# Key-tile weights added by accumulating DMA, and matmuls of one kind gathered by beat, in a two-layer graph-attention kernel

## The chip, the cores and the metric

The kernel runs on one core of a Trainium2 chip. Time is device microseconds of one launch. Three runs of the kernel before gave 4396.21, 4403.12 and 4403.44 us, so the median is 4403.12 us. The profile is that of one more execution, which took 4387.29 us; its span, from the first to the last recorded instruction, is 4385.5 us, with a mean granted TensorE clock of 0.98.

## What is computed

Two layers over `x` of shape [8, 2048, 256] (8 batches, 2048 nodes, 256 features) with one adjacency matrix of 2048 x 2048. Cut to what matters here:

```python
# layer 0: four heads of 64; a softmax over each chunk of 256 keys, the chunks' results are added
scores = einsum("bhnd,bhjcd->bhnjc", q, k) / sqrt(64)
scores = where(mask == 0, -10, clip(scores, -10, 10))
ctx = einsum("bhnjc,bhjcd->bhnd", softmax(scores, axis=-1), v)
x = layernorm(x + layernorm(ctx @ Wo.T + bo + x) * gamma + beta)
# layer 1: graph attention, one head
Wh = x @ W
e = where(adj or eye, leaky_relu(s_i[:, None] + s_j[None, :], 0.2), -inf)
x = layernorm(x + elu(softmax(e, axis=-1) @ Wh))
```

## The kernel before

**Layer 0** works on blocks of 512 queries (`ib`, 4 per batch) and chunks of 256 keys (`j`, 8 per block), 256 chunks in all. A chunk has two halves, one key tile of 128 each, and a half is a *beat*. The loop over `J` and `half` writes out the order of every engine by hand: each engine executes what the program gives it in that order. Keys lie on the partitions, queries along the free axis. In its beat a key tile gets its scores (line 899, two PSUM tiles `sc` of two heads each, from a ring of two), the cap by the mask on VectorE (909) and the exponential on ScalarE (912), which makes the two weight tiles `e` of 128 x 1024. The four `e` of a chunk come from a ring of eight.

One chunk later the weights of chunk `prev` are used (928): a matmul with `ones` as stationary operand gives the sum over the keys (part 2), two with the values give the halves of the head's features (parts 0 and 1). Each takes both key tiles (`i` = 0, 1), accumulates in PSUM, and uses a strip of 32 columns per head. The even beat does parts 2 and 0, the odd beat part 1. The results go to SBUF by ScalarE (936 to `un`, 942 to `ds`), both through a PSUM ring of two, `m`. The sums go by DMA to a compact tile (944), are inverted on VectorE (950), go to DRAM and come back spread over the partitions (952, 956); two beats after the sums `scaled` multiplies `un` (963, VectorE) and adds it to `ctxT` (964, GpSimd).

**Layer 1** of batch b runs beside layer 0 of batch b+1. A *step* is one key tile of a block of 512 queries; 16 steps make a block, four blocks a batch. A step has five parts on four engines: `low` (714, ScalarE), `leaky` (718, VectorE), `edges` (723, VectorE), `weights` (727, an exponential on ScalarE, then the add to `acc` on GpSimd, 736) and `product` (746, four matmuls into the one PSUM tile `us`; for the last batch 761). After the 16th product ScalarE copies `us` to `hx` (773), and the next block's first product has to wait for that copy. A step's `w` comes from a ring of five. `begin_beat` adds 1.5 steps of credit per beat (`RATE`), so beats alternate between one new step and two; the parts are spread so that `low` is in beat n, `leaky` and `edges` in n+1, `weights` and `product` in n+2. Within a beat the order is: `weights`, `low`, `leaky` (in `begin_beat`), then scores, caps and exponentials of layer 0, then `edges`, then the matmuls on `prev`, then `end_beat`: the products, one turn of each generator in `ahead` (the preludes: `Wh`, and the row maxima in `half_max`, 438) and `fins` (projections, the ends of blocks), and the agenda.

Layer 0 ends before layer 1 does. The last loop, `while agenda or fins or ...`, then runs beats with no scores in them: one step a beat for what is left of batch 6 and all 64 steps of batch 7.

All DMAs are issued by SyncE. GpSimd's queue has only arithmetic.

Of the kernel before, what the change touches and what calls it, by code (L numbers as in the profile page):

```python
# [9 lines left out]
F32 = mybir.dt.float32  # L10
# [4 lines left out]
ALU = mybir.AluOpType  # L15
# [4 lines left out]
P = 128  # L20
# [8 lines left out]
def tile_adj_attention__then__gat(  # L29
# [35 lines left out]
    nc = tc.nc  # L65
    B, N, F = x.shape
    H, D = 4, 64
# [3 lines left out]
    IB = 512  # L71
    NIB = N // IB
# [17 lines left out]
    four = ctx.enter_context(tc.tile_pool(name="four", bufs=4))  # L90
    five = ctx.enter_context(tc.tile_pool(name="five", bufs=5))
    eight = ctx.enter_context(tc.tile_pool(name="eight", bufs=8))
# [136 lines left out]
    for n in range(2):  # L229
        t = one.tile([P, F], F32, tag=("hx", "ex")[n], name=f"a_bc{n}")  # L230
        nc.sync.dma_start(out=t, in_=a[n * F : (n + 1) * F, :].rearrange("f o -> (f o)").partition_broadcast(P))
        a_bc.append(t)
# [355 lines left out]
    def fin1(b, ib, hx, acc):  # L588

        hr = one.tile([P, TPB, F], F32, tag="hr", name=f"hr{b}_{ib}")  # L590
        nc.sync.dma_start(out=hr, in_=h_d[b, ib])
        yield


        pr = ps_m.tile([P, TPB], F32, tag="m", name=f"pr{b}_{ib}")
        for t in range(TPB):
            nc.tensor.matmul(pr[:, t : t + 1], acc[:, ts(t, P)], ones[:, 0:1], start=True, stop=True)
        r = two.tile([P, TPB], F32, tag="r1", name=f"r1{b}_{ib}")
        nc.vector.reciprocal(r, pr)
        for t in range(TPB):  # L600
            nc.scalar.activation(hx[:, t, :], hx[:, t, :], AF.Identity, bias=ones[:, 0:1], scale=r[:, t : t + 1])
        ex = one.tile([P, TPB, F], F32, tag="ex", name=f"ex{b}_{ib}")
        nc.scalar.activation(ex, hx, AF.Exp, bias=shifts[:, 1:2])
        yield
        nc.vector.scalar_tensor_tensor(hx, ex, 1.0, hx, ALU.min, ALU.max)
        nc.gpsimd.tensor_add(hx, hx, hr)
        yield
        mv, rstd = yield from stats(hx, f"c{b}_{ib}")
        yield
        normalize(hx, mv, rstd, f"c{b}_{ib}")  # L610
        nc.sync.dma_start(out=out[b, ts(ib, IB), :].rearrange("(t p) f -> p t f", p=P), in_=hx)

    def fin1_last(b, ib, hx):
# [3 lines left out]
        nc.sync.dma_start(out=hr, in_=h_d[b, ib])  # L617
        ex = one.tile([P, TPB, F], F32, tag="ex", name=f"ex{b}_{ib}")
        st = two.tile([P, TPB, 6], F32, tag="st", name=f"st_c{b}_{ib}")
# [84 lines left out]
    class Step:  # L704
# [6 lines left out]
        def low(self):  # L711
            k, c = self.k, self.c
            self.w = five.tile([P, IB], F32, tag="w", name=f"w{self.name}")
            nc.scalar.activation(self.w, k["ab"][:, 1, :], AF.Identity, bias=k["sj"][:, 1, c : c + 1])  # L714
# [98 lines left out]
    def at(when, fn):  # L813
        agenda.setdefault(when, []).append(fn)

    def begin_beat(rate):
        nonlocal l1_live, credit, lows, edged, weighted, leaking
        weighted, edged = edged, []
        for s in weighted:
            s.weights()  # L820
        leaking, lows = lows, []
        credit = min(credit + rate, 2.0)
        while l1_live and credit >= 1.0:
            s = next(l1, False)
            if s is False:
                l1_live = False
            elif s is None:
                break
            else:
                credit -= 1.0  # L830
                lows.append(s)
                s.low()
        for s in leaking:
            s.leaky()

    def middle_of_beat():
        nonlocal edged
        for s in leaking:
            s.edges()
        edged = leaking  # L840

    def end_beat():

        nonlocal weighted
        if beat < 2 * NIB * NCH or beat >= 2 * total:
            for fn in agenda.pop(beat, []):
                fn()
        for s in weighted:
            s.product()
        weighted = []  # L850
        for gens in (ahead, fins) if beat < 2 * total else (fins, ahead):
# [17 lines left out]
    fins.append(far_made())  # L869

    prev = None
    mk0 = {}
    for J in range(total + 1):
        b, ib, j = J // (NIB * NCH), J // NCH % NIB, J % NCH
        live = J < total
        if live and j == 0:
            ctxT = one.tile([P, 2, IB], F32, tag="ctx", name=f"ctxT{b}_{ib}")
        cur = {"b": b, "ib": ib, "j": j, "es": [], "ctxT": ctxT, "v": vs[min(b, B - 1)], "name": f"{b}_{ib}_{j}"}
        for half in range(2):
            c = 2 * j + half  # L880
            if live:
# [6 lines left out]
                if c % HT == 1:  # L888
                    n = (b * NIB + ib) * 2 + c // HT + 1
                    nb, nib, nhf = n // (2 * NIB), n // 2 % NIB, n % 2  # L890
                    if 0 < nb < B:
                        mk0[nb, nib, nhf] = mask_block(0, nib, nhf, f"{nb}_{nib}_{nhf}")
            begin_beat(RATE if b < B - 1 else LAST_RATE)
            if live:
                scs = []
                for hp in range(NPAIR):
                    sc = ps_s.tile([P, 2, IB], F32, tag="sc", name=f"sc{b}_{ib}_{c}_{hp}")
                    for h in range(2):
# [6 lines left out]
                        )  # L905
                    scs.append(sc)
                cap = mk[:, c % HT, :].unsqueeze(1).to_broadcast([P, 2, IB])
                for hp in range(NPAIR):
# [6 lines left out]

            early = J < NIB * NCH
            if prev is not None:
                if half == 0:

                    pool, tag = (one, "hr") if early and J % 3 == 2 else (two, "un")  # L920
                    prev["un"] = pool.tile([P, 2, IB], F32, tag=tag, name=f"un{prev['name']}")
                for part in ((2, 0), (1,))[half]:
                    m = ps_m.tile([P, IB], F32, tag="m", name=f"u{prev['name']}_{part}")
                    for i in range(2):
                        pc = 2 * prev["j"] + i
                        for h in range(H):
                            f0 = h * D + part * DH
                            nc.tensor.matmul(  # L928
                                m[h * DH : (h + 1) * DH, :],
                                prev["v"][pc // TPB][:, pc % TPB, f0 : f0 + DH] if part < 2 else ones[:, 0:DH],  # L930
                                prev["es"][2 * i + h // 2][:, h % 2, :],
                                start=(i == 0),
                                stop=(i == 1),
                            )
                    if part < 2:
                        nc.scalar.copy(prev["un"][:, part, :], m)  # L936
                    else:

                        ds = two.tile([P, IB], F32, tag="ds", name=f"ds{prev['name']}")
                        nc.scalar.copy(ds, m)  # L942
                        dc = two.tile([P, IB // DH], F32, tag="dc", name=f"dc{prev['name']}")
                        nc.sync.dma_start(
                            out=dc, in_=ds.rearrange("(h m) (n w) -> h m n w", m=DH, n=DH)[:, 0, :, :]
                        )
                        prev["dc"] = dc

                        def inverse(p=prev):
                            nc.vector.reciprocal(p["dc"], p["dc"])  # L950
                            p["rd"] = dram3.tile([H, IB], F32, tag="rd", name=f"rd{p['name']}")
                            nc.sync.dma_start(out=p["rd"].rearrange("h (m w) -> (h m) w", m=DH), in_=p["dc"])

                        def spread(p=prev):
                            p["r"] = two.tile([P, IB], F32, tag="r", name=f"r{p['name']}")
                            nc.sync.dma_start(out=p["r"], in_=p["rd"].unsqueeze(1).to_broadcast([H, DH, IB]))

                        def scaled(p=prev):
                            r2 = p["r"].unsqueeze(1).to_broadcast([P, 2, IB])
                            if p["j"] == 0:  # L960
                                nc.vector.tensor_mul(p["ctxT"], p["un"], r2)
                            else:
                                nc.vector.tensor_mul(p["un"], p["un"], r2)  # L963
                                nc.gpsimd.tensor_add(p["ctxT"], p["ctxT"], p["un"])  # L964
                            if p["j"] == NCH - 1:
                                ctx_done[p["b"], p["ib"]] = beat
                            if p["j"] == NCH - 3:
                                fins.append(fin(p["b"], p["ib"], p["ctxT"]))

                        lag = 1 if early else 0  # L970
                        at(beat + lag, inverse)
                        at(beat + lag, spread)
                        at(beat + 2 + 2 * lag, scaled)

            end_beat()
            if half == 1:

# [8 lines left out]
    while agenda or fins or ahead or l1_live or l1_open():  # L986
        begin_beat(1.0)
        middle_of_beat()
        end_beat()
        beat += 1  # L990
# [44 lines left out]
```

## Time and profile before

| | us |
|---|---|
| median of three runs | 4403.12 |
| the profiled execution | 4387.29 |
| its span | 4385.5 |
| PE busy | 4064.2 (93%) |
| VectorE (DVE) busy | 3417.7 (78%) |
| ScalarE (ACT) busy | 2564.4 (58%) |
| GpSimd (POOL) busy | 1760.5 (40%) |
| DMA, share of the 16 engines' span | 30.5% for queue q1, which SyncE feeds |

An fp32 matmul of the program is two MATMUL and two LDWEIGHTS instructions in the profile, so the scores of a beat (four matmuls) are eight. Busy time is time with an instruction in flight; PE's instructions overlap, so a group's mean duration is longer than its share of the busy time. A timeline gives start, duration, engine, line, operation, tiles and count of each stretch of like instructions; in brackets stands how long the engine was idle before and what released it.

### The profile page before, as it was taken

How to read it: one execution, taken by the hardware profiler on the slowest of the kernel's cores; microseconds unless marked ns; L12 is line 12 of the kernel's file. 1: busy time of each engine (PE TensorE's matmuls, PEld its weight loads, DVE VectorE, ACT ScalarE, POOL GpSimd, SP SyncE). 2: the span in 40 equal slices, each digit the busy share in tenths (PEclk: the TensorE clock that was granted, in tenths of full speed). 3: DMA queues.
4: the chain of work that ended last, by engine and by line, in shares of the span. 5: the costliest groups of instructions: out<-in, count | busy, mean ns of one | idle time of the engine just before them, and what ended most of it. 6: DMA issues, size and time to landing. Idle time of an engine off the chain costs nothing. (4 is left out here: it accounts for less than half of the span.)

```text
span 4385.5 us, 61171 instructions
## 1 busy us (share of the span) xinstructions
PE 4064.2 (93%) x23053; PEld 1907.6 (43%) x23053; DVE 3417.7 (78%) x4530; ACT 2564.4 (58%) x3842; POOL 1760.5 (40%) x901
## 2 busy tenths in 40 slices
PE   8889989999999999999899999999999999899767
PEld 3223334454344534454344543445434454344456
DVE  5876589965998669976699766996579965888777
ACT  5655556665566556666566665566556665555546
POOL 0222235543455334444245442554325542354420
PEclk9999999999999999999999999999999999999889
DMA  5554232222332233321333223232232222322321
GB/s 166 182 163 149 71 115 86 83 73 89 99 90 81 64 107 102 100 75 51 105 102 98 74 74 105 85 95 78 70 106 85 89 78 67 115 83 80 123 73 58
DMA packets 257641, 415.63 MB, mean 95 GB/s; under 512 B 85440, under 2 KB 120512, under 8 KB 256448
## 3 DMA queue, kind: packets, MB, share of 16 engines
q1 hardware_dynamic: 257344, 411.71, 30.5%
q8 instruction: 181, 2.97, 0.3%
q14 instruction: 116, 0.95, 0.1%
HBM read 340.66 MB, written 68.88 MB: 93 GB/s over the span
## 5 line engine op out<-in xcount | busy, mean ns | idle before, releaser
L912 ACT ACTIVATE e<-sc 128x1024 f32<-128x1024 f32 x1024 | 1034.2, 1020 | 1049.9 <-DVE sc L909 1006.7
L909 DVE SCALAR_TENSOR_TENSOR sc<-sc,mk 128x1024 f32<-128x1024 f32 x1024 | 1206.7, 1223 | 538.3 <-PE sc L899 352.6
L899 PE MATMUL sc<-qT,kT 64*128 64x512 f32 x4096 | 1060.4, 633 | 86.7 <-ACT e L912 86.2
L964 POOL TENSOR_TENSOR ctxT<-ctxT,un 128x1024 f32<-128x1024 f32 x224 | 568.5, 2538 | 1145.3 <-DVE un L963 1007.0
L928 PE MATMUL u<-e,v 128*32 128x512 f32 x8192 | 980.9, 597 | 0.0
L746 PE MATMUL us<-wh,w 128*128 128x256 f32 x3584 | 878.6, 395 | 81.9 <-ACT w L727 60.4
L746 PEld LDWEIGHTS us<-wh,w 128*128 128x128 f32 x3584 | 667.7, 193 | 422.2 <-ACT w L727 110.7
L736 POOL TENSOR_TENSOR acc<-acc,w 128x512 f32<-128x512 f32 x392 | 601.7, 1535 | 544.9 <-ACT w L727 534.4
L899 PEld LDWEIGHTS sc<-qT,kT 64*128 64x128 f32 x4096 | 347.2, 189 | 611.6 <-ACT e L912 281.8
L718 DVE SCALAR_TENSOR_TENSOR w<-ab,sj,w 128x512 f32<-128x512 f32 x512 | 571.5, 1137 | 4.6 <-ACT w L714 4.5
L928 PEld LDWEIGHTS u<-e,v 128*32 128x32 f32 x8192 | 240.6, 110 | 659.7 <-issue 543.9
L928 PE MATMUL u<-e,ones 128*32 128x512 f32 x4096 | 497.5, 604 | 0.0
L723 DVE TENSOR_TENSOR w<-w,mk 128x512 f32<-128x512 f32 x512 | 458.6, 917 | 37.1 <-DMA mk<-mask 34.6
L438 DVE CUSTOM_DVE_ANT_0 fb<-sj_row,fb 128x1024 bf16<-128x1024 f32 x240 | 387.8, 1626 | 2.3 <-DMA fb<-far 2.3
L714 ACT ACTIVATE w<-ab,sj 128x512 f32<-128x512 f32 x512 | 352.2, 714 | 8.7 <-POOL acc L734 5.4
L727 ACT ACTIVATE w<-w 128x512 f32<-128x512 f32 x512 | 308.8, 629 | 75.9 <-DVE w L723 75.3
L936 ACT COPY un<-u 128x512 f32<-128x512 f32 x512 | 300.5, 587 | 66.5 <-PE u L928 57.6
L963 DVE TENSOR_TENSOR un<-un,r 128x1024 f32<-128x1024 f32 x224 | 278.1, 1242 | 42.2 <-DMA r<-rd 36.7
L928 PEld LDWEIGHTS u<-e,ones 128*32 128x32 f32 x4096 | 107.8, 110 | 356.5 <-issue 305.4
L950 DVE RECIPROCAL dc<-dc 128x16 f32<-128x16 f32 x256 | 63.9, 249 | 149.8 <-DMA dc<-ds 134.0
L942 ACT COPY ds<-u 128x512 f32<-128x512 f32 x256 | 148.5, 580 | 3.0 <-PE u L928 2.5
L349 POOL TENSOR_TENSOR y<-x,bo_bc 128x1024 f32<-128x1024 f32 x32 | 77.6, 2426 | 163.6 <-DMA x<-in_x_dram 103.0
(112 smaller groups left out, 3114.7 us busy)
## 6 DMA issues: line engine op xcount, KB each, us to landing
r<-rd SPq DMA_DIRECT2D x256, 256.0 KB
mk<-mask SPq DMA_DIRECT2D x120, 512.0 KB
fb<-far SPq DMA_DIRECT2D x240, 256.0 KB
xT_k<-in_xT_dram SPq DMA_DIRECT2D x32, 512.0 KB
raw<-in_adjT_dram SPq DMA_DIRECT2D x32, 512.0 KB
rawf<-in_adj_dram SPq DMA_DIRECT2D x32, 512.0 KB
x<-in_x_dram SPq DMA_DIRECT2D x32, 512.0 KB
h_d<-y SPq DMA_DIRECT2D x32, 512.0 KB
```

The source lines that it names most:

```text
L438: nc.vector.tensor_tensor_reduce(out=fb, in0=row, in1=fb, scale=1.0, scalar=2 * FAR * 0.999, op0=ALU.add, op1=ALU.max, accum_out=dst,)
L714: nc.scalar.activation(self.w, k["ab"][:, 1, :], AF.Identity, bias=k["sj"][:, 1, c : c + 1])
L718: nc.vector.scalar_tensor_tensor(self.w, k["ab"][:, 0, :], k["sj"][:, 0, c : c + 1], self.w, ALU.add, ALU.max)
L723: nc.vector.tensor_tensor(self.w, self.w, self.k["mks"][self.c // HT][:, self.c % HT, :], ALU.min)
L727: nc.scalar.activation(self.w, self.w, AF.Exp)
L736: nc.gpsimd.tensor_add(k["acc"], k["acc"], self.w)
L746: nc.tensor.matmul(k["us"][:, t, :], self.w[:, ts(t, P)], k["wh"][c // TPB][:, c % TPB, 0:F], start=(first and t % 2 == 0), stop=last, ski ...
L899: nc.tensor.matmul(sc[:, h, :], kTs[b][c // TPB][h * D : (h + 1) * D, hp, ts(c % TPB, P)], qT[h * D : (h + 1) * D, hp, :], start=True, sto ...
L909: nc.vector.scalar_tensor_tensor(scs[hp], scs[hp], -CLIP, cap, ALU.max, ALU.min)
L912: nc.scalar.activation(e, scs[hp], AF.Exp)
L928: nc.tensor.matmul(m[h * DH : (h + 1) * DH, :], prev["v"][pc // TPB][:, pc % TPB, f0 : f0 + DH] if part < 2 else ones[:, 0:DH], prev["es"] ...
L964: nc.gpsimd.tensor_add(p["ctxT"], p["ctxT"], p["un"])
```

## The change

It concerns chunks that have layer-1 steps in hand beside them (`together`), found at the start of each even beat. For these:

- The even beat does both value parts of `prev`, key tile by key tile. After them GpSimd issues two DMAs that add the weights of the second key tile to those of the first, in place (128 x 1024 fp32 each).
- The sums of that chunk are taken one chunk later, in the next even beat behind the scores, from the added tiles alone: one key tile in place of two.
- The layer-1 products are held for the odd beat.

For all beats the layer-1 parts are ordered anew: `weights_and_lows` (first the exponentials and the adds to `acc`, then the `low` of the new steps) comes at the end of an even beat, behind the copies of `un`, and at the start of an odd beat. `leaky` and `edges` follow in `begin_beat` and `middle_of_beat`, so a `low` of an odd beat is used in that beat. The last loop calls `weights_and_lows`, `begin_beat`, `middle_of_beat` in this order, too. The rings change: `w` from five to six tiles, `un` from two and a guest in `hr` to three, `ds` from two to one; `fin1` loads `hr` later, and `ex` shares the place of `hr`.

```diff
-    def begin_beat(rate):
-        nonlocal l1_live, credit, lows, edged, weighted, leaking
-        weighted, edged = edged, []
-        for s in weighted:
+    def weights_and_lows(rate):
+        nonlocal l1_live, credit, lows, edged, weighted
+        for s in edged:
             s.weights()
-        leaking, lows = lows, []
+        weighted, edged = weighted + edged, []
         credit = min(credit + rate, 2.0)
...
                 lows.append(s)
                 s.low()
+
+    def begin_beat():
+        nonlocal lows, leaking
+        leaking, lows = lows, []
         for s in leaking:
             s.leaky()
...
-        for s in weighted:
-            s.product()
-        weighted = []
+        if products:
+            for s in weighted:
+                s.product()
+            weighted = []
...
+    def sums(p, lag):
...
+        m = ps_m.tile([P, IB], F32, tag="m", name=f"s{p['name']}")
+        tiles = 1 if p["added"] else 2
+        for i in range(tiles):
+            for h in range(H):
+                nc.tensor.matmul(
+                    m[h * DH : (h + 1) * DH, :],
+                    ones[:, 0:DH],
+                    p["es"][2 * i + h // 2][:, h % 2, :],
...
-            begin_beat(RATE if b < B - 1 else LAST_RATE)
+            early = J < NIB * NCH
+            rate = RATE if b < B - 1 else LAST_RATE
+            if half == 1:
+                weights_and_lows(rate)
+            begin_beat()
+            if half == 0:
+                together = prev is not None and live and bool(leaking or edged or weighted)
...
+            if half == 0:
+                for p in unsummed:
+                    sums(p, 0)
+                unsummed = []
...
+                    if not together:
+                        sums(prev, 1 if early else 0)
+                parts = (0, 1) if together and half == 0 else (half,) if not together else ()
...
+                for i in range(2):
+                    for part, m in zip(parts, ms):
+                        values(prev, part, m, i)
+                    if together and half == 0 and i == 1:
...
+                        for hp in range(NPAIR):
+                            nc.gpsimd.dma_start(
+                                out=prev["es"][hp], in_=prev["es"][NPAIR + hp], accum_op=ALU.add
                             )
+                        prev["added"] = True
+                        unsummed.append(prev)
+                for part, m in zip(parts, ms):
+                    nc.scalar.copy(prev["un"][:, part, :], m)
+            if half == 0:
+                weights_and_lows(rate)
+            edged = edged + leaking
-            end_beat()
+            end_beat(half == 1 or not together)
...
     while agenda or fins or ahead or l1_live or l1_open():
-        begin_beat(1.0)
+        weights_and_lows(1.0)
+        begin_beat()
         middle_of_beat()
-        end_beat()
+        edged = edged + leaking
+        end_beat(True)
         beat += 1
```

## The prediction, made before the changed kernel was run

> **What bounds the kernel now.** The page first: PE is busy 93% of the span, but the slices of its second part do not say the same everywhere.
>
> ```profile
> PE   8889989999999999999899999999999999899767
> DVE  5876589965998669976699766996579965888777
> ```
>
> DVE's digits rise to 9 and fall to 5 once per batch (some 4.7 slices), so two engines may take turns. The list of scores (line 899) in the timeline gives the batches' period, 526 us from batch 3 to batch 4 (1485.7 to 2012.5), 32 chunks. The line-746 products show which chunks have layer 1 beside them: 22 of 32, in batches 1 to 7, so 154 chunks. Busy time of the stages of one period, then of the end (columns: stretch, length, PE, PEld, DVE, ACT, POOL, clock, DMA share, GB/s):
>
> ```profile
> 1660.00:1895.00 235.00, 222.41 (x1294) 106.76 (x1286) 221.50 (x274) 146.33 (x218) 120.15 (x61) 0.99 0.33 99
> 1895.00:2065.00 170.00, 168.21 (x920) 87.07 (x920) 116.44 (x151) 102.30 (x158) 72.06 (x42) 1.00 0.20 60
> 4245.00:4373.00 128.00, 115.33 (x481) 92.01 (x481) 103.06 (x187) 86.33 (x146) 3.02 (x3) 0.96 0.19 66
> ```
>
> In 13 chunks of the first stretch, where the row maxima (438) run, PE and DVE are both at 94%: taking PE work away there leaves DVE. In the 9 chunks of the second PE is alone at 99%. In the third, the end, one layer-1 step comes every 128/60 = 2.13 us.
>
> A plain chunk with three steps, on PE:
>
> ```profile
> 2353.81 1.99 PE L899 MATMUL sc<-qT,kT 64*128 64x512 f32 x8
> ...
> 2355.72 1.92 PE L928 MATMUL u<-e,ones 128*32 128x512 f32 x16
> ...
> 2357.46 1.90 PE L928 MATMUL u<-e,v 128*32 128x512 f32 x16
> ...
> 2359.29 2.00 PE L746 MATMUL us<-wh,w 128*128 128x256 f32 x8
> ...
> 2361.22 1.99 PE L899 MATMUL sc<-qT,kT 64*128 64x512 f32 x8
> ...
> 2363.14 1.92 PE L928 MATMUL u<-e,v 128*32 128x512 f32 x16
> ...
> 2364.99 3.72 PE L746 MATMUL us<-wh,w 128*128 128x256 f32 x16
> ...
> 2368.64 1.99 PE L899 MATMUL sc<-qT,kT 64*128 64x512 f32 x8
> ```
>
> Start to start, PE never rests: 14.83 us.
>
> **What PE is spared.** Sixteen sum instructions become eight: 1.74/2 = 0.87 us. Entering a kind of matmul also costs: the two-part `u` group takes 3.57 us, the one-part 1.85, so 1.72 per part and 0.13 for entry; the products take 3.65 against 1.93, so 1.72 per step and 0.21 for entry. The Trainium skill, "TensorEngine Tiling (Array Packing)", section Key Properties, says that a change of tiling mode drains the array; it names no price, the rows do. The order goes from six kinds a chunk to four (scores, sums with values; scores, products), which drops one `u` and one `us` entry: 0.34 us. Together 1.21, and PE's chunk becomes 13.62 us. Over 154 chunks that would be 186 us, if PE were the bound everywhere.
>
> **What takes its place inside a chunk.** `low` now stands behind the copies of `un`, these behind the values, and `leaky` of all three steps ahead of the odd beat's caps. That closes a ring. From the end of the even scores: sums 0.87 + 0.13, values 3.44, hop and last copy 0.07 + 0.58, three exponentials at 0.54 (start to start), the first `low` 0.71, three `leaky`, two caps 2.35, hop and exponential of the second pair 0.1 + 1.02, hop and scores of that pair 0.1 + 0.96. Without `leaky` 11.95 us. Single `leaky` instructions of the timeline take 0.72 us alone (102 of them) and 1.40 with a POOL instruction in flight at their start (139); the mean of the row is 1.137. This is where the rule that speaks against the change comes in: the Trainium skill, "SBUF — State Buffer", section Who interferes with whom, says a DVE instruction with two SBUF inputs contends with a GpSimd instruction that reads SBUF, and `leaky` is one. The adds to `acc` (1.27 each) start as soon as the exponentials end, and now meet `leaky`. By the rule the ring is 11.95 + 4.20 = 16.2 us, by `leaky` alone 14.1, by the mean 15.4. I take 15.4, since the first add can pass while DVE waits for `low`.
>
> So a PE-bound plain chunk goes from 14.8 to 15.4; one with a projection (3.5 us or more on PE) stays PE's and gains 1.21. In the nine chunks of the second stretch six have such work, two are plain, one has few steps: -7.3 + 1.1 - 0.4 = -6.6 us a batch, **-46 us** for seven. In the 13 chunks of the first stretch (mean 17.1 us) DVE's work stays what it is. Ends: -1.21 x 91 = -110, if DVE's contention shrinks as PE's work does, and +91 if each chunk loses 1 us to the ring. I take **0**.
>
> **Block changes.** `us` is one PSUM tile; the copy to `hx` stands on ACT behind the odd beat's exponentials. Today:
>
> ```profile
> PE us L746 <- ACT hx L773: 21.5, 7, 3.9
> ```
>
> 21.5 us in 7 waits. With three products in one run, the 16th step ends inside the run at two of a batch's three inner boundaries. In the ring's time the second exponential ends 14.3 us after the even scores, the copy (1.01) at 15.4. The first product ends near 8.4. If the boundary follows it, two products (3.45) and scores (1.92) come behind the copy: 20.8 against 15.4, +5.4. If it follows the second: +3.7. 14 such boundaries x 4.55 = 64, less 21.5: **+42 us**; from 0, if the stall falls into DVE's backlog, to 64.
>
> **The end.** There `leaky` used the `low` of the beat before; now it needs that of its own beat, which stands on ACT behind the exponential of the step before, which needs that step's `edges`. The trace shows this very chain once, where it happened to run without slack:
>
> ```profile
> 4298.11 0.70 ACT L714 ACTIVATE w<-ab,sj 128x512 f32<-128x512 f32 x1
> ...
> 4298.85 0.75 DVE L718 SCALAR_TENSOR_TENSOR w<-ab,sj,w 128x512 f32<-128x512 f32 x1 [0.64 <-ACT w L714]
> ...
> 4299.64 0.69 DVE L723 TENSOR_TENSOR w<-w,mk 128x512 f32<-128x512 f32 x1
> ...
> 4300.36 0.63 ACT L727 ACTIVATE w<-w 128x512 f32<-128x512 f32 x1 [0.41 <-DVE w L723]
> 4300.90 0.71 ACT L714 ACTIVATE w<-ab,sj 128x512 f32<-128x512 f32 x1
> ```
>
> From `low` to `low` 2.79 us. At one step a beat, 60 steps x (2.79 - 2.13) = **+40 us**. The ends of blocks (`fin1_last`) fit into DVE's and ACT's gaps of the chain. Bounds: 20 to 55.
>
> **The accumulating DMAs.** No row has one; GpSimd issues none today. Room: from the values' end to the sums, 15.4 - 4.4 = 11 us. Nearest rows: the 8 KB dc<-ds takes 1.81 us in the chain of waits, and in the busiest 20 us (4140 to 4160) 258 GB/s went at a share of 0.73, so 353 GB/s at full share. Two tiles are 1.05 MB: 3.0 us in one pass; if the add reads its target too, two passes, 5.9, over the 0.7 that others leave 8.5; with 1.8 for landing, 4.8 to 10.3. The fit of "DMA: Bandwidth & Descriptors", section Anatomy of one DMA — SWDGE (gpsimd) path (2.0 us plus the bytes over 436,000 a us), would make it 6.4, one after the other. Cost taken: 0, hidden by the odd beat; ends 0 and what rival 2 says. Issuing 308 DMAs on POOL has no row either (SP's issues take 0.3 to 0.56 us each): POOL is busy half of either stretch, and behind the two waiting issues stand only the adds to `acc`, whose exponentials come later. 0, ends 0 and +1 us in each of the 91 DVE-bound chunks, should the issue keep DVE off SBUF as POOL's adds do.
>
> The later sums move dc, rd and r by a chunk; `scaled` moves with them, and nothing but the output projection waits for it, 2 beats later. `hr` in `fin1` is loaded a beat before its use, on SP behind `ex`. 0, ends -5 and +15 over the run.
>
> **Sum.** -46 + 0 + 42 + 40 = +36 us on the profiled 4387.29, so 4423; the three runs lie higher, median 4403.12, and there the same +0.8% gives **4440**.
>
> **Rivals.**
> 1. *PE's saving carries (faster).* If `edges`, now issued where POOL is idle, and `leaky` run at 0.72, the ring is 14.1: plain chunks gain 0.7, and the first stretch gains half of PE's 1.21. -9 a batch and -0.6 x 91: -63 - 55 + 20 (stalls half absorbed) + 40 = -58, so 4345. It decides once the ring is below 14.8 us. For: DVE's singles at 0.72 to 0.75 wherever POOL rests. Against: the `acc` adds sit right there.
> 2. *The DMA lands late.* From 11 us on, the chunk is the landing time + 4.4. At three passes, 12.7 + 1.8 = 14.5, a chunk takes 18.9 at least; of the 22 some 17 are shorter, by 2.5 us on average: +42 a batch, +290, 4730. For: no row excludes it. Against: two passes fit.
>    That `together` holds in fewer chunks than 154 would shrink every term but the end's.
> 3. *The ring is contended.* 16.2 us, +1 in the DVE-bound chunks: plain chunks +1.4, so -34 in the second stretch, +91 + 42 + 40: +139, 4540.
>
> **How the numbers follow.** Forecast 0.45, its own range 4408 to 4500; rival 1 0.25, rival 2 0.16, rival 3 0.14. About 0.2% (9 us) is what a measurement can tell from no change. Faster: all but a little of rival 1, and a part of the forecast's lower side, 0.26; same 0.08; slower 0.66. The range 4335 to 4650 leaves out a part of rival 1 and the worse half of rival 2.
>
> **What would show it.** Right: chunks with projections 1.2 us shorter, plain ones near 15.4 with DVE waiting for line-714 `low`; PE waiting for `hx` 5 and 4 us, twice a batch; steps of the end at 2.8 us; sums that do not wait for a DMA. Wrong: plain chunks below 14.5, or PE waiting at the sums.

## The result, and the profile after

Four runs of the changed kernel gave 4995.81 to 5018.11 us, median 5010.1; four of the kernel before 4396.21 to 4403.44, median 4403.18. The ratio is 1.1379 (95% interval 1.1351 to 1.1407): the change costs some 607 us. The forecast was 4440, and the time lies far above its range.

The slices of the page of the changed kernel, to be read beside the two shown of before, with the granted TensorE clock:

```profile
PE   8889877898788887889888888888987889888666
DVE  6875678665776667766677556776577765777665
PEclk9999989899899998999989998899998999989789
```

PE's row of nines is gone, and DVE no longer swings to 9: where two engines took turns as the bound, now neither is full. The clock falls below 9 all along the run; its mean is 0.926 where it was 0.980. Sums of the page say the same: PE idles 840 us of the span (4994.0 less 4154.0) where it idled 321, and is busy 90 us *longer*, with fewer instructions.

The stages of one period and the end, in the columns of the table shown of before. The first row holds the same chunks of batch 3 as the 235 us of before, the second the nine behind them, the third the products of the last batch:

```profile
1834.00:2107.00 273.00, 220.68 (x1139) 101.76 (x1139) 208.66 (x252) 141.91 (x211) 120.48 (x79) 0.90 0.52 128
2107.00:2304.00 197.00, 173.55 (x873) 92.02 (x873) 132.03 (x165) 105.98 (x160) 94.25 (x62) 0.96 0.44 104
4782.00:4979.00 197.00, 135.50 (x522) 98.39 (x522) 123.09 (x219) 97.52 (x164) 6.89 (x5) 0.95 0.15 48
```

The first stretch grew from 235 to 273 us. DVE was busy 94% of it and is now at 76%; PE executes 155 matmul instructions fewer (104 of them sums; the others have moved to neighbouring chunks) in the same busy time, at a clock of 0.90 where it was 0.99. The second grew from 170 to 197. By the starts of the scores, averaged over batches 2 to 5, a batch went from 527.4 to 609.3 us: its 21 chunks with layer 1 from 377.6 to 444.2, its 11 others from 149.8 to 165.1. (The same places of a batch are compared in every kernel; one of the 11 still holds one or two steps.) From the last scores to the last matmul it was 263 us and is 341.

One plain chunk of batch 4 (on PE it has nothing but scores, sums, values and products) in the timeline of the changed kernel, from even scores to even scores, PE, ACT, POOL and DVE together:

```profile
2507.66 1.99 PE L969 MATMUL sc<-qT,kT 64*128 64x512 f32 x8
...
2510.46 3.71 PE L881 MATMUL u<-e,v 128*32 128x512 f32 x32
...
2514.11 1.99 PE L969 MATMUL sc<-qT,kT 64*128 64x512 f32 x8
2514.24 0.59 ACT L1012 COPY un<-u 128x512 f32<-128x512 f32 x1 [0.22 <-PE u L881]
2514.73 1.67 ACT L728 ACTIVATE w<-w 128x512 f32<-128x512 f32 x3
2515.51 4.30 POOL L737 TENSOR_TENSOR acc<-acc,w 128x512 f32<-128x512 f32 x3 [0.75 <-ACT w L728]
2516.03 5.45 PE L747 MATMUL us<-wh,w 128*128 128x256 f32 x24
2516.30 1.94 ACT L715 ACTIVATE w<-ab,sj 128x512 f32<-128x512 f32 x3
2517.04 6.07 DVE L719 SCALAR_TENSOR_TENSOR w<-ab,sj,w 128x512 f32<-128x512 f32 x3 [3.34 <-ACT w L715]
2519.77 2.79 POOL L924 TENSOR_TENSOR ctxT<-ctxT,un 128x1024 f32<-128x1024 f32 x1
2523.04 2.35 DVE L985 SCALAR_TENSOR_TENSOR sc<-sc,mk 128x1024 f32<-128x1024 f32 x2
2524.29 2.15 ACT L988 ACTIVATE e<-sc 128x1024 f32<-128x1024 f32 x2 [6.06 <-DVE sc L985]
...
2525.37 3.79 PE L969 MATMUL sc<-qT,kT 64*128 64x512 f32 x8 [3.90 <-ACT e L988]
```

This is the ring of the prediction, link by link: values, copies, exponentials, `low`, three `leaky`, caps, exponential, scores. It takes 17.71 us. DVE waits 3.34 us for the first `low`; then three `leaky` take 6.07 us, 2.02 each, while GpSimd has adds in flight (its two lines). Taken one by one in the trace, they last 1.64, 1.75 and 2.83 us. GpSimd's second and third add to `acc` and the larger add of `scaled` (924) end at 2518.14, 2519.81 and 2522.57, and each `leaky` ends some 0.55 us after one of these: the two engines take turns. The forecast had 1.137 each, 1.40 at worst. The odd beat's caps stand behind them; PE has been through with its products for 3.90 us when the exponential lets it go on, and the eight scores instructions that follow take 3.79 us where eight took 1.99. The clock column (the third from the right) says why, in the first part of the wait, in its last part, and in the scores behind it:

```profile
2521.50:2523.50 2.00, 0.00 (x0) 0.00 (x0) 2.00 (x2) 0.00 (x0) 1.07 (x1) 1.00 1.02 274
2523.70:2525.30 1.60, 0.00 (x0) 0.00 (x0) 1.60 (x2) 1.01 (x1) 0.00 (x0) 0.50 0.81 229
2525.37:2529.20 3.83, 3.83 (x12) 1.25 (x16) 3.59 (x10) 1.02 (x1) 0.00 (x0) 0.50 0.08 27
```

Some 2.2 us after PE's last product (2521.48) the granted clock went to one half, and it stayed there while PE worked again.

Waits of the kernel before, then of the changed kernel (engine, tile and line, what it waited for: us in total, times, longest):

```profile
DVE w L718 <- ACT w L714: 4.5, 9, 1.3
...
PE sc L899 <- ACT e L912: 86.2, 57, 6.3
```

```profile
DVE w L719 <- ACT w L715: 530.5, 273, 6.1
...
PE sc L969 <- ACT e L988: 424.2, 139, 7.2
...
PE us L747 <- ACT hx L774: 93.4, 14, 9.7
```

The third was 21.5 us before, in 7 waits. The 14 block changes are where the prediction put them.

The accumulating DMAs, from the list of DMA issues (number, KB each, median us from issue to landing):

```profile
e<-e POOLq DMA_DIRECT2D x302, 512.0 KB, 6.4
```

The two of a chunk together take 8.0 us from the first issue to the last landing (median of 151 pairs), 11.2 at most. 302 are two in each of 151 chunks, so `together` holds about where it was expected (154 chunks), and among what PE's sums wait for there is no DMA.

### The profile page after: what moved, and what is told of

It reads as the page before. It is cut to its first block, busy times and chain, and to the rows that moved or that the text cites. A ratio compares the mean times of both kernels' runs of the same rounds, so it can differ in the third digit from the quotient of the medians.

```text
span 4994.0 us, 59349 instructions
## 1 busy us (share of the span) xinstructions
PE 4154.0 (83%) x21845; PEld 1935.9 (39%) x21845; DVE 3468.9 (69%) x4530; ACT 2582.1 (52%) x3842; POOL 1941.6 (39%) x1203
## 5 line engine op out<-in xcount | busy, mean ns | idle before, releaser
L969 PE MATMUL sc<-qT,kT 64*128 64x512 f32 x4096 | 1195.5, 701 | 458.0 <-ACT e L988 424.2
L719 DVE SCALAR_TENSOR_TENSOR w<-ab,sj,w 128x512 f32<-128x512 f32 x512 | 773.4, 1542 | 534.2 <-ACT w L715 530.5
L747 PE MATMUL us<-wh,w 128*128 128x256 f32 x3584 | 862.2, 397 | 133.2 <-ACT hx L774 93.4
L969 PEld LDWEIGHTS sc<-qT,kT 64*128 64x128 f32 x4096 | 377.7, 205 | 1072.9 <-ACT e L988 691.4
L1006 POOL DMA_DIRECT2D e<-e x302 | 269.5, 1033 | 1196.6 <-PE u L881 1094.4
L737 POOL TENSOR_TENSOR acc<-acc,w 128x512 f32<-128x512 f32 x392 | 549.2, 1401 | 196.6 <-ACT w L728 177.2
L724 DVE TENSOR_TENSOR w<-w,mk 128x512 f32<-128x512 f32 x512 | 382.7, 787 | 79.5 <-DMA mk<-mask 76.7
L905 ACT COPY ds<-s 128x512 f32<-128x512 f32 x256 | 149.4, 583 | 547.8 <-PE s L897 392.5
L897 PE MATMUL s<-e,ones 128*32 128x512 f32 x2888 | 406.9, 666 | 14.6 <-DVE y L364 13.5
L438 DVE CUSTOM_DVE_ANT_0 fb<-sj_row,fb 128x1024 bf16<-128x1024 f32 x240 | 319.3, 1341 | 0.0
L897 PEld LDWEIGHTS s<-e,ones 128*32 128x32 f32 x2888 | 72.3, 115 | 333.7 <-issue 274.5
```

What stands on the lines that cost most here:

```text
L719: nc.vector.scalar_tensor_tensor(self.w, k["ab"][:, 0, :], k["sj"][:, 0, c : c + 1], self.w, ALU.add, ALU.max)
L724: nc.vector.tensor_tensor(self.w, self.w, self.k["mks"][self.c // HT][:, self.c % HT, :], ALU.min)
L737: nc.gpsimd.tensor_add(k["acc"], k["acc"], self.w)
L747: nc.tensor.matmul(k["us"][:, t, :], self.w[:, ts(t, P)], k["wh"][c // TPB][:, c % TPB, 0:F], start=(first and t % 2 == 0), stop=last, ski ...
L897: nc.tensor.matmul(m[h * DH : (h + 1) * DH, :], ones[:, 0:DH], p["es"][2 * i + h // 2][:, h % 2, :], start=(i == 0), stop=(i == tiles - 1),)
L969: nc.tensor.matmul(sc[:, h, :], kTs[b][c // TPB][h * D : (h + 1) * D, hp, ts(c % TPB, P)], qT[h * D : (h + 1) * D, hp, :], start=True, sto ...
```

## The experiments

In the expectations "ring" or "Theory A" is the order of layer 1, A1 the work that ScalarE has between the `low` of a chunk, A2 `leaky` contended by GpSimd, S the lateness of the sums, H the holding of the products for the odd beat, and D the accumulating DMAs. Of each kernel not stated otherwise the rest is that of the changed kernel. "21" and "11" are the us of a batch's chunks with and without layer 1, as above.

### Is it the order or the DMAs?

**No accumulating DMAs**, the late sums over both key tiles:

```diff
-                        for hp in range(NPAIR):
-                            nc.gpsimd.dma_start(out=prev["es"][hp], in_=prev["es"][NPAIR + hp], accum_op=ALU.add)
-                        prev["added"] = True
```

> The changed kernel without the accumulating DMAs: sums still one chunk late, but over both key tiles. Theory A (the ring low - leaky - caps - exponentials - scores - values - copies - low sets the length of a chunk): the DMAs are off the ring and 0.87 us of sums is added to it in 151 chunks, so 5010 to 5140 us. Rival B (the DMAs: landing, or their issue on GpSimd, hold the chunk): clearly below the changed kernel, 4450 to 4700 us.

Measured: 5077.18 us (one run), 21: 452.2. That is in the ring's range. Without the DMAs it is slower still, so neither their landing nor their issue is what costs the 607 us.

**The old order** of layer 1, in the chunks and in the last loop; DMAs, late sums and held products stay:

```diff
-    def begin_beat():
+    def begin_beat(rate):
         nonlocal lows, leaking
-        leaking, lows = lows, []
+        held, lows = lows, []
+        weights_and_lows(rate)
+        leaking = held
...
-            if half == 0:
-                weights_and_lows(rate)
```

> The changed kernel with the layer-1 order of the kernel before (exponentials, then low, then leaky for the low of the beat before, all at the start of every beat, also in the last loop); accumulating DMAs, late sums, values in even beats and products in odd ones stay. Theory A: the ring is open, so the time falls to that of the kernel before or below it, 4250 to 4420 us. Rival B (DMAs): stays above 4700 us. Rival C (holding the products for the odd beat, with the stall for hx at block changes, is the cost): stays above 4600 us.

4525.76 us, ratio to before 1.0283 (1.0266 to 1.03); 21: 383.0, 11: 164.6. The time lies in none of the three ranges: the order carries 484 of the 607 us, but 123 are left that the ring theory did not expect.

**The old order in the last loop only:**

> The changed kernel with the order of the kernel before in the last loop alone. Theory A: the end (64 steps of the last batch, 198 us in the changed kernel against 148 before) is back at about 148 us and the rest stays, so 4930 to 4970 us. If the longer end has another cause than leaky needing the low of its own beat: 4990 to 5010 us.

4947.23 us (one run): the last loop is 63 of the 484; the stretch behind the last scores is 57 us shorter.

**The new order only** (`together = False`, so old sums and values, no DMAs, products in every beat):

> The changed kernel with no chunk taken as together: sums over both tiles at once, values one part a beat, products in every beat, no accumulating DMA; the new layer-1 order stays in all beats. Theory A: nearly the whole loss is the order's, 4850 to 5150 us. Rivals B and C (DMAs, held products): 4400 to 4550 us, the end's 50 us being all that is left.

5108.1 us (one run), 21: 465.5, 11: 161.7 (9.1 of these 11.9 us more are in the one place of the 11 that has steps). It is in the ring's range. The order needs no help from the rest of the change.

### Which part of the ring?

**All `low` of a chunk in the even beat** (`weights_and_lows(2 * rate, 3.0)` there, none in the odd one):

> The changed kernel with all of a chunk's low in the even beat, behind the exponentials, and none in the odd one; leaky for all of them still opens the odd beat, so the ring stays closed. Theory A1 (the ring is longer than forecast because ScalarE's work for block ends and projections stands between the low of the even and of the odd beat): chunks with layer 1 lose 2 to 4 us, 4600 to 4850 us. Theory A2 (because leaky meets GpSimd's adds): 4960 to 5040 us.

4945.72 us (one run), 21: 433.7. Only 64 us come back, in neither range and nearest to A2's: work between the `low` of two beats is a small part.

**The ring cut.** All `low` of a chunk stand in the even beat, as in the kernel above, behind the copies, but their `leaky` and `edges` wait for the next even beat:

```diff
-    def begin_beat():
+    def begin_beat(mine=True):
         nonlocal lows, leaking
-        leaking, lows = lows, []
+        leaking, lows = (lows, []) if mine else ([], lows)
...
-            begin_beat()
+            begin_beat(half == 0)
...
             if half == 0:
-                weights_and_lows(rate)
+                weights_and_lows(2 * rate, 3.0)
```

> The changed kernel with the ring cut: all lows of a chunk stand behind the even beat's copies of un, as before, but their leaky and edges wait for the next even beat, 20 us later, so that no cap stands behind a leaky whose low is fresh. The accumulating DMAs, late sums, held products, the last loop and the place of the lows and step exponentials on ScalarE stay. Ring theory (the way from low through leaky to the caps of the same beat is what makes a chunk with layer 1 last 20 us): such chunks come back near the 383 us per 21 of the old order, and with the last loop's 60 us left the time is 4580 to 4650. Rival, contention alone (leaky takes 1.54 us because GpSimd's adds meet it): at most 3 x 0.4 us per chunk come back, 25 us a batch, so 4830 to 4900. Rival, ScalarE's place alone (step exponentials and lows between the copies and the odd beat's exponentials delay the latter): nothing comes back, 4930 to 5020.

4632.9 us, ratio 1.0542 (1.0515 to 1.057), 21: 388.1. 377 us are gone, inside the ring theory's numbers and far from both rivals'; against the kernel above, which differs in the place of `leaky` and `edges` alone, it is 313. A plain chunk of batch 4, in the timeline of this kernel:

```profile
2103.54 1.99 PE L967 MATMUL sc<-qT,kT 64*128 64x512 f32 x8
...
2111.23 2.37 DVE L983 SCALAR_TENSOR_TENSOR sc<-sc,mk 128x1024 f32<-128x1024 f32 x2 [0.91 <-ACT w L728]
...
2112.18 1.94 ACT L715 ACTIVATE w<-ab,sj 128x512 f32<-128x512 f32 x3
...
2113.51 5.49 DVE L719 SCALAR_TENSOR_TENSOR w<-ab,sj,w 128x512 f32<-128x512 f32 x3
...
2117.28 1.99 PE L967 MATMUL sc<-qT,kT 64*128 64x512 f32 x8
```

Here `leaky` is nearly as contended (1.83 us each). By the order on either engine these three still belong to the three `low` just above them and follow at once, not 20 us later as had been expected. But the odd beat's caps now stand ahead of them on VectorE, so no exponential and no scores wait for them. PE never rests: 13.74 us from scores to scores. The forecast for PE alone was 13.62.

**A shorter ring**: the `leaky` of the odd beat's `low` move to the next even beat, those of the even beat's stay.

```diff
-            if half == 1:
-                weights_and_lows(rate)
             begin_beat()
+            if half == 1:
+                weights_and_lows(rate)
```

> The changed kernel with a shorter ring: the lows keep their places (1.5 on average at the end of the even beat, 1.5 at the start of the odd one), but the leaky and edges of the odd beat's lows move to the next even beat. The ring then holds one or two leaky in place of three, and does not hold the odd beat's low. Ring theory: some 1.5 x 1.54 us of leaky and about 1 us of low and hop leave a chunk's 20 us, so 2.3 to 3.3 us in 21 chunks of 7 batches: 4520 to 4670 if all of it counts, 4700 to 4800 if PE's or VectorE's own work takes over in half of the chunks. Contention alone: half of the leaky meet other GpSimd work, 4900 to 4960. ScalarE's place alone: 4980 to 5030.

4643.04 us, ratio 1.0566 (1.0533 to 1.0598), 21: 390.3. It is in the theory's range: halving what the ring holds on VectorE gives back nearly as much as cutting it.

**GpSimd's adds to `acc` left out**, in the changed kernel, and in the kernel before as a control:

> The changed kernel without GpSimd's adds of the step weights to acc (in batches 0 to 6 only the weights of each block's second step are kept, plus one; the output changes). If GpSimd's adds are what stretches three leaky in a row to 6 us and with them the ring: leaky comes back to 0.75 to 1.1 us, the ring loses 2.5 to 3.5 us in 151 chunks: 4480 to 4650. If the ring's length comes from elsewhere (work between the lows on ScalarE, row maxima ahead of the caps, PE at half clock after each wait): 4850 to 5000.

> The kernel before with the same adds left out, as the control: its leaky lie where nothing waits in the same beat. If contention alone costs VectorE's time: 1.1 us in the 91 chunks that VectorE bounds, 4290 to 4340. If PE's queue bounds it: 4370 to 4400. Either way much less than in the changed kernel, if the ring is what makes the contention count.

4831.81 us for the changed kernel, 178 less than with the adds; 4343.18 for the kernel before (ratio 0.9872, 0.9857 to 0.9887), 56 less. The first lies in neither range, the second 3 us above that of contention: in the changed kernel contention is more than nothing and less than all. (One add per block stays.) The same chunk of batch 4 as above, without the adds:

```profile
2432.48 1.99 PE L967 MATMUL sc<-qT,kT 64*128 64x512 f32 x8
...
2441.11 1.93 ACT L715 ACTIVATE w<-ab,sj 128x512 f32<-128x512 f32 x3
2441.86 2.08 DVE L719 SCALAR_TENSOR_TENSOR w<-ab,sj,w 128x512 f32<-128x512 f32 x3 [3.34 <-ACT w L715]
2443.85 2.36 DVE L983 SCALAR_TENSOR_TENSOR sc<-sc,mk 128x1024 f32<-128x1024 f32 x2
...
2446.22 2.23 PE L967 MATMUL sc<-qT,kT 64*128 64x512 f32 x8
```

`leaky` 2.08 us in place of 6.07, the chunk 13.74 in place of 17.71: the 3.97 us that the chunk loses are the 3.99 that `leaky` gained. In a plain chunk contention is the whole excess over PE's time. In the others it isn't: DVE still waits 544.5 us in all for `low`, and 21 chunks with layer 1 end at 420.3 us in this kernel, 37 above the old order's. Of these 37 us, 18.6 lie in the two chunks of a batch where a block changes, and 6.7 in the first chunk of a batch with layer 1. PE's wait for `hx` is hardly less without the adds (89.3 us in 14 waits), so contention does not make it. What else delays the ring in such chunks was not separated.

### What is left with the old order

**The rings alone** (`w` of six, `un` of three, `ds` of one, the later `hr`; old order, nothing together, products in every beat):

> What is left of the change once the order, the held products, the gathered values, the late sums and the accumulating DMAs are all taken back: the rings (w of six, un of three, ds of one, hr loaded a beat later and in the place of ex). Theory (late sums cost what the old order leaves over): no cost, 4385 to 4420, chunks without layer 1 near 150 us per 11, tail near 277. Rival (the rings: the single ds, or hr's late load): 4470 or more, with 160 to 165 and 290 to 298.

4400.18 us, ratio 1.0013 (1.0006 to 1.0021); 21: 380.7, 11: 150.1. Some 6 us.

**Late sums alone** (that kernel, with the sums over both key tiles a chunk later where layer 1 runs beside):

> Late sums alone: the old order, products in every beat, one value part in each beat as before, no accumulating DMAs; only the sums (over both key tiles) stand a chunk later in chunks with layer 1 beside them. Theory (the lateness of dc, rd, r, scaled and the ends of blocks costs the 100 us): 4480 to 4510, with 160 to 165 us per 11 chunks without layer 1 and a tail 20 us longer. Rival (both value parts in the even beat are what costs): 4395 to 4420.

4483.85 us, ratio 1.0192 (1.0176 to 1.0207), 11: 164.7, the stretch behind the last scores 20 us longer than with the rings alone. So 1.8%, some 79 us, for nothing but the lateness. It falls where nothing had been expected to wait: in the 11 chunks without layer 1 and at the end. The traces of the two kernels show the work of a block's end one chunk later, and PE waiting. Over the run PE waits longer for layer 0's exponentials, first with the rings alone, then with late sums:

```profile
PE sc L969 <- ACT e L988: 89.6, 60, 6.3
```

```profile
PE sc L969 <- ACT e L988: 146.9, 69, 6.3
```

At the output projection it waits 32.1 us for a copy of `un`, where it waited 2.9. In all, PE idles 51 us more and is busy 42 us more, with the same instructions.

**Both value parts in the even beat as well**, still without DMAs:

> The old order with products in every beat, values gathered in the even beat and sums a chunk late, but without the accumulating DMAs, so that the late sums take both key tiles (0.87 us of PE more per chunk). If the DMAs' cost is what keeps PE's saving from showing (they take 4 us a batch net where products are held): 4470 to 4490, faster than the 4500 with them. If PE's saving counts here: 4520 to 4620. If late sums alone cost nothing: 4400.

4501.17 us, ratio 1.0249 (1.0228 to 1.027). A further 0.6%; the time lies in none of the ranges.

**And the DMAs** (the old-order kernel with products in every beat):

> e2 with the products in every beat; both value parts in the even beat, accumulating DMAs and late sums stay. Theory H: 4420 to 4470 us. Theories S and D: 4510 to 4560 us (one entry of the products more per chunk, 0.21 us x 151 = 32 us at most).

4500.51 us (one run). PE is busy 4004.2 us where it was 4092.1 without the DMAs, and the time is the same: what PE is spared turns into waiting. The time is in the range of neither theory. **With products held** and no DMAs:

> e2 without the accumulating DMAs; the sums stay a chunk late, over both tiles. Theory D: 4430 to 4490 us. Theories S and H: 4520 to 4600 us, as 0.87 us of sums a chunk come back (at most 131 us, where PE is the bound).

4495.68 us (one run), against 4525.76 with them, again in neither range. So there the DMAs cost some 0.6%, by one run, for a reason that stays open.

**Sums half a chunk later** in place of a whole one: the kernel with DMAs and without held products, its sums from the added tiles in the odd beat, behind the scores.

```diff
             middle_of_beat()
+            if half == 1:
+                for p in unsummed:
+                    sums(p, 0)
+                unsummed = []
```

> The old order with products in every beat and the accumulating DMAs, but the sums from the added tiles taken in the odd beat of the same chunk, behind its scores, half a chunk after the values in place of a whole one. Theory (what the late sums shift, the chain dc, rd, r, scaled and the ends of blocks behind it, is what costs): half of the 100 us left over comes back, 4430 to 4470. Rival (the DMA's 6.4 us is now too late and PE waits at the sums): 4500 to 4650, with waits of PE m for the DMA in the trace. If neither costs, and PE's 0.87 us count: below 4397.

5072.54 us, ratio 1.1545 (1.1523 to 1.1566). The rival's wait is there, and costs more than its range had. The first of PE's waits in this kernel:

```profile
PE s L899 <- DMA e<-e: 410.2, 176, 7.5
```

The DMA that "costs nothing" a chunk ahead of its use stops PE in 102 of the 151 chunks when it is needed half a chunk later.

**Sums at once over both tiles**, in the old-order kernel with values gathered and products held, without DMAs:

> e2 (layer-1 order of before, 4526 us) without accumulating DMAs and without late sums: sums over both tiles at once; both value parts in the even beat and the products held for the odd one stay. Theory S (what is left over the kernel before, 127 us, comes from the late sums: block ends and preludes start a chunk later, and their loads stand ahead of the DMA of the sums on SyncE): 4380 to 4450 us. Theory H (holding the products): 4490 to 4560 us. Theory D (the DMAs, by their issue on GpSimd): 4400 to 4470 us.

4658.28 us (one run), above all three ranges; 11: 150.4, 21: 417.2. The 11 chunks are back at the value of before, as S has it. The 21 pay for something else, in this kernel's waits:

```profile
PE u L883 <- ACT ds L907: 262.4, 151, 6.5
```

Sums and two value parts need three tiles of a PSUM ring of two, so the values wait in all 151 chunks for the copy of the sums, which stands behind the exponentials. So this kernel can't say what gathering and holding cost without late sums.

**The sums of a block's chunks 5 and 7 at once** (counted from 0; old order, products held), and **six of a block's eight chunks gathered**, those two as before (old order, products in every beat):

> e2, but the sums of the sixth and eighth chunk of a query block are taken at once over both tiles, so that the block's end starts when it did before; the other six chunks keep DMA and late sums. Theory S: 4410 to 4460 us. Theories H and D: 4510 to 4560 us.

> The layer-1 order of the kernel before, products in every beat; both value parts in one beat, accumulating DMAs and late sums only for six of the eight chunks of a query block, while the sixth and the eighth are done exactly as before the change (sums at once, one value part a beat). Theory S (late sums push block ends and preludes a chunk back): the 11 chunks of a batch that have no layer 1 fall from 165 to 150 us and the end from 298 to 277, 4360 to 4415 us in all. Theory D (the DMAs cost what they spare): 4430 to 4480 us.

4532.6 us (one run) and 4511.4 (ratio 1.0266, 1.0249 to 1.0283). Both miss: 11 falls to 157.8 and 157.6, half of the way, and 21 rises to 391.8 and 386.9. So it is not only the end of a block that is late. Which of the things behind the sums (reciprocal, spread, `scaled`, block ends, their loads on SyncE's queue) makes PE wait was not taken apart further. None of the kernels with the whole computation beats the one before.

## Why the prediction was wrong

**The step that failed is "What takes its place inside a chunk".** It found the ring, named its links in order and the rule that makes `leaky` contend, and then gave it 15.4 us, 16.2 at most. It is 17.7 in the plain chunk shown, and three things were missed:

- *`leaky` at the row's mean.* 1.137 us was an average over places where GpSimd often rests. In the ring the three follow the very exponentials that release three adds to `acc`, with `scaled`'s add behind them: 2.02 each. The reason given for the low value is true (the first add passes while DVE waits for `low`), but three more follow. Even the upper bound, 1.40, was an average over whatever GpSimd had in flight. Among these instructions of the kernel before are some of 0.66 to 0.75 us beside GpSimd's short operations on `rstd`, and others of 1.75 behind an add to `acc` (median of 52). The excess of 3 x (2.02 - 1.137) = 2.65 us on 15.4 makes 18.0; the trace shows 17.7.
- *The first stretch at 0.* "DVE's work stays what it is" is right in the main (208.7 us busy, 221.5 before), but a ring puts a wait into the middle of DVE's order. While DVE waits 3.3 us for `low`, the work behind it can't start. Being bound by an engine was taken as being covered by it.
- *PE's answer to waiting.* All links were taken at full clock. After a wait of over 3 us PE nearly always starts at half speed (see below), which lengthens the very scores that the ring waits for: 3.79 us in place of 1.99 behind the chunk shown.

With the block changes, and with what else delays the ring in the chunks that are not plain, it comes to 444.2 - 377.6 = 66.6 us a batch, 466 in seven, against a forecast of -4 for the stretches and the block changes. 61.2 of the 66.6 go with the old order (383.0).

**What PE is spared**: right, 13.74 us a chunk against 13.62, wherever the ring is out of the way. It was worth nothing in the time.

**Block changes**: the mechanism and the 14 places are right; 6.7 us each (93.4/14) in place of 4.55. A contended ring is not the reason, since it is 6.4 without the adds; with the old order and the products still held it is 2.2 (28.5 us in 13 waits). Why the new order makes it so long stays open.

**The end.** The chain of the last loop, in the changed kernel's timeline:

```profile
4863.46 0.71 ACT L715 ACTIVATE w<-ab,sj 128x512 f32<-128x512 f32 x1
...
4864.20 0.75 DVE L719 SCALAR_TENSOR_TENSOR w<-ab,sj,w 128x512 f32<-128x512 f32 x1 [0.76 <-ACT w L715]
4864.99 0.69 DVE L724 TENSOR_TENSOR w<-w,mk 128x512 f32<-128x512 f32 x1
...
4865.71 0.63 ACT L728 ACTIVATE w<-w 128x512 f32<-128x512 f32 x1 [1.54 <-DVE w L724]
...
4866.25 0.70 ACT L715 ACTIVATE w<-ab,sj 128x512 f32<-128x512 f32 x1
```

From `low` to `low` 2.79 us, to the hundredth as forecast. 57 to 63 us in place of 40. 60 steps were counted; the loop holds the 64 of batch 7 and 22 left of batch 6 (176 line-747 instructions, eight a step), and 86 x 0.66 would be 57.

**The accumulating DMAs**: PE's sums do not wait for them, as forecast; the two land in 8.0 us, inside the 11 us of room. That each takes 6.4, the figure that the fit gave in the prediction, is chance: there it stood for both, one after the other. Rival 2 falls by the waits and by the kernel without DMAs, which is slower.

**The later sums**: wrong. 0, ends -5 and +15, against some 79 us. The chain behind the sums was asked who waits for its last link, and not what PE has to wait for when a block's end comes a chunk later: 57 us more for layer 0's exponentials, 29 more at the output projection.

**The rivals.** Number 3, the contended ring, had the right mechanism at too small a size: 1.40 us for each `leaky`, and 1 us for each chunk that VectorE bounded. Number 1 needed a ring below 14.8 us. Without GpSimd's adds a plain chunk is there (13.74), and the kernel is still slower than before: the other chunks, the late sums and the last loop keep their cost.

## What to carry to other kernels

Before work is gathered by kind, write out the ring that the new order closes, from an engine's instruction back to itself, and price each link with what runs *beside it in the new order*, for its whole length; a row's mean is the price in the old one. A ring through three in-order engines also stops the work queued behind its waits, so an engine that is 94% busy does not hide it. Where an order must put a producer late, let its consumer run a turn later: here that slack was worth 313 us, more than the 186 that the change could have gained.

## What the hardware showed besides

**Half speed after a wait.** In the records of both kernels the granted clock is either 1.00 or 0.50. From 15 us on it is 0.50 in 34 stretches before, 180 us together, and in 145 stretches after, 738 us. The runs of eight scores instructions in the timeline, sorted by how long PE was idle ahead of them:

| idle before, us | before: runs, median us | after: runs, median us |
|---|---|---|
| under 1 | 479, 1.99 | 371, 1.99 |
| 1 to 2 | 22, 2.26 | 35, 2.26 |
| 2 to 3 | 6, 3.38 | 38, 3.10 |
| over 3 | 5, 2.94 to 3.79 | 68, of them 67 at 2.83 to 3.79 |

From 3 us of idleness on, the next scores run at close to half speed, and from 2 us on mostly (27 of the 38 took over 2.5 us). The Trainium skill, "TensorE: Matmul & The Clock Gate", section HAM oscillation — how this bites in real kernels, asks for no PE gaps above some 3.4 us. By that rule the runs behind gaps of 2 to 3 us would be at full speed; here most were not, so for this kernel the table decides. It is a second payment for each wait: the scores group is busy 1195.5 us for 4096 instructions where it was 1060.4. So a wait on PE is not worth its length alone.

**`leaky` beside GpSimd.** 0.69 us each without an add in flight (2.08 for three), 2.02 with adds in flight nearly throughout: a factor of 2.9, on an instruction with two SBUF inputs. An add in flight is not the price; its end is. In the changed kernel 209 `leaky` of over 0.9 us began beside an add to `acc`, and 59 beside `scaled`'s add; all but 5 of them ended some 0.55 us after that add. In the kernel before, 35 began within some 0.04 us of a `scaled` add and took 0.66, and that add took 2.9 us, where it took 2.36 with the `leaky` behind it.
